# A two-layer graph attention kernel: rows of x stored by turns in layer 1 and loaded in one piece in layer 2, no rows for missing edges in layer 1, and a ring of 29 slots for 28

## The chip, the core and the metric

The kernel runs on one core of a Trainium2 chip. The metric is the device time of one execution in microseconds; the kernel before has a median of 5479.95 us over 14 runs (5473.43 to 5489.02). The names of the engines are those of the profile: PE (TensorE; PEld is its weight load), DVE (VectorE), ACT (ScalarE), POOL (GpSimd) and SP (SyncE, which here only issues DMAs).

## What is computed

Two graph attention layers on 10,000 nodes and 170,000 given edges (each node's self loop is among them, and the reference adds another), then a residual and a normalisation:

```python
def gat_conv(x, edge_index, W, a_src, a_dst, bias, heads, out_ch, concat):
    ei = _add_self_loops(edge_index, n)
    src, dst = (ei[0], ei[1])
    xl = (x @ W).reshape(n, heads, out_ch)
    alpha_src = jnp.einsum('nhc,hc->nh', xl, a_src)
    alpha_dst = jnp.einsum('nhc,hc->nh', xl, a_dst)
    e = jax.nn.leaky_relu(alpha_src[src] + alpha_dst[dst], 0.2)
    # softmax of e over the edges of each dst
    msg = xl[src] * alpha[:, :, None]
    out = jax.ops.segment_sum(msg, dst, num_segments=n)
...
h = gat_conv(x, edge_index, W1, a_src1, a_dst1, b1, 4 heads of 256, True)
h1 = relu(layer_norm(h, g1, be1)) + (x @ Wr1 + br1)
h = gat_conv(h1, edge_index, W2, a_src2, a_dst2, b2, 1 head of 768, False)
out = layernorm(x + layer_norm(h, g2, be2) + (h1 @ Wr2 + br2))
```

x is 10000 x 768, h1 is 10000 x 1024; everything is in float32.

## The kernel before, in words

Three stages follow one another. The first (to 899 us) multiplies x by W1 and writes table1: for each node a row of 1033 numbers, namely 1024 of x @ W1, four logit parts as a source, four as a destination, and one number R1 - 1 that is the node's place in the order below. `prepare` runs between these products. It sorts the nodes by their number of edges, cuts them into 79 tiles of 128, and lists for each tile as many slots as its fullest node needs: slot k of a tile holds, for each of the 128 nodes, the table row of its k-th edge (slot 0 is the node itself). A node with fewer edges has in the slots left over the number of one extra row (`none`), whose logits are -1e30, so that its weight is zero. The tiles have 8 to 41 slots, 1377 in all. `TURNS` is the order of the tiles: every second one from the smallest to the largest, then the others back to small.

Layer 1 (`ordered_layer1`, 899 to 3419 us) goes through the tiles. The rows of a slot come by one indirect DMA from POOL (`gather`, L418, 128 rows) into a ring of RING1 = 28 slots (class `Ring`; `fetch` issues the gather of a slot as soon as the program has weighed the slot that was in its place). `logits` (L467 to L478) adds the source parts of a tile's slots to the destination part, with one DVE instruction for each unbroken stretch of the ring, and takes the exponential on ACT (L475); in layer 1 it then copies the number R1 - 1 of each row into `slots` on ACT (L478), which is the list that layer 2 gathers by. `normalised` (L485 to L491) makes the softmax. The rows are then weighed and summed: the first few slots by PE with diagonal matrices (L709), the others by DVE, one in four wholly (L508) and three in four after ACT has scaled them (L497, then L504). `weights_of(t + 1)` does the next tile's logits and first diagonals before the last LEAD = 3 slots of tile t are weighed, where SLOTS[t + 1] + LEAD fits in the ring. So DVE waits at L467 for the last gather of the next tile with three weighings behind it. Beside this PE transposes the tile's rows of x (L572, which ACT copies out at L575), multiplies them by Wr1, normalises the tile before (L550 to L566, with ACT's square root at L554), and multiplies its h by W2. SP stores the row of layer 2 (table2, L730) and hT (h1_d, L777). The tile's rows of x, 128 x 768, come by a gather by node from POOL (`fetch_x`) into one of two buffers `xt`; it is issued at the end of a tile, for the tile two further on.

Layer 2 (`ordered_layer2`, 3419 to 5475 us) has the same order, with a ring of 38 slots and rows of 770 numbers. A tile's own rows lie together in table2, so slot 0 comes by a direct load from SP (L445) and the others by gathers from POOL. DVE weighs 512 columns (L508), PE the other 256 (L859, L860). `residual(t + 1)` begins the PE work of tile t (L871 takes x, L874 hT); it needs hT, which SP loads from h1_d (L835), and the tile's rows of x, which POOL gathers a second time. Both are asked for in the middle of the weighing of the tile two before. The result is scattered by node (L893) with a bounds check, since the last tile has nodes beyond the 10,000. For the one tile that the ring can't hold whole (41 slots), `attend_parts` works in parts, and the x of the tile two further on is asked for after it.

Each engine runs its instructions in the order in which the program gives them (`manual_schedule`), and POOL and SP issue their DMAs in that order too: a DMA whose wait isn't over holds back all those behind it on the same engine. POOL's DMAs use eight semaphores in turn, so each waits for the one eight before it.

Of the kernel before, what the change touches and what calls it, by code (L numbers as in the profile page):

```python
# [34 lines left out]
P = 128  # L35
# [9 lines left out]
G = 4  # L45
RING1 = 28
RING2 = 38
# [31 lines left out]
def gnn_kernel(ctx, tc, x, x_cols, src, dst, src_col, dst_col, W1, a_src1, a_dst1, b1, g1, be1, Wr1, br1,  # L79
# [27 lines left out]
    res2 = dram.tile([NP, C2], F32, name="res2")  # L107
    h1_d = dram.tile([NT, P, C1], F32, name="h1_d")
    shift = dram.tile([1, C2], F32, name="shift")
    order_d = [dram.tile([NP, 4], I32, name=f"order{i}_d") for i in range(LISTS)]  # L110
# [77 lines left out]
    def prepare():  # L188

        with tc.tile_pool(name="prep", bufs=1, side="right") as pool, \  # L190
# [108 lines left out]
            nc.vector.tensor_sub(base, base, each)  # L299
            rank = pool.tile([P, NT], F32, name="rank")  # L300
            to = pool.tile([P, NT], I32, name="to")
            written = 0
# [34 lines left out]
            with nc.allow_non_contiguous_dma(reason="16 bytes a node"):  # L337
                for to, d in zip([sorted_] + others, order_d):
                    nc.sync.dma_start(to, d.rearrange("(t p) f -> p t f", p=P))
                    yield  # L340
                nc.sync.dma_start(table1[:NP, R1 - 1:].rearrange("(p j) r -> p (j r)", p=P), rank)
                yield
# [91 lines left out]
    class Ring:  # L434

        def __init__(self, pool, table, row, size, own):
            self.table, self.size, self.own, self.issued = table, size, own, 0
            self.rows = pool.tile([P, size, row], F32, name="ring")  # L440

        def fetch(self, upto):
            for q in range(self.issued, min(upto, TOTAL)):
                if q in self.own:
                    nc.sync.dma_start(self.slot(q), self.table[self.own[q] * P:(self.own[q] + 1) * P, :])  # L445
                else:
                    gather(self.slot(q), self.table[:, :], slots[:, q:q + 1])
                self.issued = q + 1
# [12 lines left out]
    def logits(small, ring, lo, hi, ad, heads, c, top=None):  # L461


        n = hi - lo
        e = small.tile([P, ring.size, heads], F32, name="e")[:, :n]
        for a, b, rows in ring.parts(lo, hi):
            nc.vector.tensor_tensor(e[:, a - lo:b - lo], rows[:, :, c:c + heads],  # L467
                                    ad[:, None, :].to_broadcast([P, b - a, heads]), op=OP.add)
# [6 lines left out]
        nc.scalar.activation(e, e, AF.Exp)  # L475
        if not ring.own:
            for a, b, rows in ring.parts(lo, hi):
                nc.scalar.copy(slots[:, a:b], rows[:, :, R1 - 1])  # L478
        return e, new
# [111 lines left out]
    with tc.tile_pool(name="w1", bufs=1) as w1p, tc.tile_pool(name="l1", bufs=2) as io, \  # L591
# [16 lines left out]
        nc.vector.memset(none[:, C1:], -BIG)  # L608
        nc.vector.memset(none[:, R1 - 1:], float(NP))
        nc.scalar.dma_start(table1[NP:NP + 1, :], none)  # L610
# [6 lines left out]
        def weight_steps():  # L617
# [8 lines left out]
            load(w2, W2)  # L626
            for i, a in enumerate((a_src2, a_dst2)):
# [16 lines left out]
        for t in range(NT):  # L644
            p = product(xTs.pop(t), w1, C1)
            row = io.tile([P, R1], F32, name="row")
            nc.scalar.copy(row[:, :C1], p[:, :C1])  # L647
            for i, vec in enumerate((as_b, ad_b)):
                m = io.tile([P, C1], F32, name="scr")
# [18 lines left out]
    def ordered_layer1():  # L668
        nonlocal ps_big
        with tc.tile_pool(name="b1", bufs=1) as pool, tc.tile_pool(name="small1", bufs=2) as small, \  # L670
# [6 lines left out]
            def fetch_x(t):  # L677
                xt = pool.tile([P, D0], F32, name="xt", bufs=2)
                gather(xt, x[:, :], nodes(t))
                return xt  # L680

            xs = {t: fetch_x(t) for t in range(min(2, NT))}
            ring.fetch(RING1)
# [7 lines left out]
            def weights_of(t):  # L691

                n, m = SLOTS[t], on_pe(t)
                e, _ = logits(small, ring, FIRST[t], FIRST[t] + n, ring.slot(FIRST[t])[:, C1 + H1:C1 + 2 * H1], H1, C1)
                yield e
# [36 lines left out]
            for t in range(NT + 1):  # L732
# [47 lines left out]
                if last:  # L780
                    events.append((first + 2, to_layer2))

                def due(k):
                    while events and events[0][0] <= k:
                        events.pop(0)[1]()

                if live and not whole:
                    due(n)
                    acc = ps_acc.tile([P, 2 * BANK], F32, name="acc")
                    ad = small.tile([P, H1], F32, name="ad")  # L790
                    nc.vector.tensor_copy(ad, ring.slot(FIRST[t])[:, C1 + H1:C1 + 2 * H1])
                    attend_parts(small, ring, acc, acc, ad, None, H1, DH1, t)
# [15 lines left out]
                if live:  # L808
                    last = r, acc
                    if t + 2 < NT:  # L810
                        xs[t + 2] = fetch_x(t + 2)
            store(NT - 1)

    def ordered_layer2():
        nonlocal ps_big
        with tc.tile_pool(name="b2", bufs=1) as pool, tc.tile_pool(name="small2", bufs=2) as small, \
# [28 lines left out]
            def weights_of(t):  # L845
# [3 lines left out]
                ad = small.tile([P, H2], F32, name="ad")  # L849
                nc.vector.tensor_add(ad, ring.slot(FIRST[t])[:, C2 + H2:], lift)  # L850
                e, _ = logits(small, ring, FIRST[t], FIRST[t] + n, ad, H2, C2)
# [52 lines left out]
            for t in range(NT):  # L904
# [4 lines left out]
                if not whole(t):  # L909
                    for _ in last:  # L910
                        pass
                    ad = small.tile([P, H2], F32, name="ad")
                    nc.vector.tensor_add(ad, ring.slot(FIRST[t])[:, C2 + H2:], lift)
                    attend_parts(small, ring, h, h, ad, b2_b, H2, DH2, t)
# [33 lines left out]
    def general_path():  # L948
# [82 lines left out]
        def attend_chunks(keep, work, small, lists, table, row, heads, dh, t):  # L1031
# [6 lines left out]
            top = keep.tile([P, heads], F32, name="top")  # L1038
            nc.vector.tensor_copy(top, acc[:, c:c + heads])
# [3 lines left out]
            nc.vector.tensor_copy(adm[:, :heads], acc[:, c + heads:c + 2 * heads])  # L1043
            tmp = small.tile([P, heads], F32, name="tmp")
# [6 lines left out]
            with tc.For_i(lo, hi, G) as i:  # L1051
# [19 lines left out]
                for g in range(0, G, zg):  # L1071
                    z = work.tile([P, zg, heads, P], F32, name="z")
                    nc.vector.tensor_tensor(
                        z, off[:, g:g + zg, None, :].to_broadcast([P, zg, heads, P]),
                        xg[:, g:g + zg, c:c + heads, None].to_broadcast([P, zg, heads, P]), op=OP.add)
                    pz = ps_tr.tile([P, BANK // P, P], F32, name="tr")
# [20 lines left out]
                e = small.tile([P, G, heads], F32, name="ge")  # L1097
                nc.vector.tensor_add(e, xg[:, :, c:c + heads], sel[:, :, :heads])
                leaky(e, e)
# [117 lines left out]
```

## Time and profile before

| | |
|---|---|
| median of 14 runs | 5479.95 us |
| the profiled execution's own time | 5476.48 us |
| its span, first to last instruction | 5474.7 us |
| mean granted TensorE clock | 0.939 |
| busy: PE, DVE, ACT, POOL | 4750.9, 4328.1, 3149.0, 3247.0 us |
| gathers of ring slots (L418) | 2675, mean 969 ns on POOL |
| gathers of x, layer 1 and layer 2 | 79 of mean 966 ns, 79 of mean 963 ns |
| moved by the DMA engines | 1581.74 MB, mean 289 GB/s |

A row of the groups of instructions gives the line, the engine, the operation, what it writes and reads, how often, its busy time and mean duration, and then the idle time of its engine just before such instructions, with those that ended it. A row of the waits gives the waiting instruction, what it waited for, and the sum, number and longest of the waits. In the windows the busy time of each engine is given for a stretch of the span. A POOL row of a gather covers the issuing alone; the transfer follows, and the table of DMA issues gives its median time to landing (5.3 us for the x gathers of layer 1, 5.4 for those of layer 2). The slices of the page show 311 to 366 GB/s through most of both layers.

### The profile page before, as it was taken

What the parts mean: (1) busy time and instruction counts of PE and PEld (TensorE: products, weight loads), DVE (VectorE), ACT (ScalarE), POOL (GpSimd) and SP (SyncE); (2) the same over time, 40 slices, a digit from 0 to 9 for tenths busy, and PEclk for the clock granted to TensorE, in tenths of its full rate; (3) what the DMA queues carried; (4) which work ended last, traced back from release to release, by engine and by line L of the source; (5) the groups of instructions that cost most, each with busy time, mean ns of one, the idle gap of its engine ahead of it and who ended that gap; (6) DMA issues with size and microseconds to landing.
All of it is one profiled execution on the core that took longest, in us unless ns stands there. A gap on an engine that the chain in (4) does not pass through costs nothing. (4 is left out here: it accounts for less than half of the span.)

```text
span 5474.7 us, 58297 instructions
## 1 busy us (share of the span) xinstructions
PE 4750.9 (87%) x15032; PEld 2828.1 (52%) x15032; DVE 4328.1 (79%) x7766; ACT 3149.0 (58%) x8255; POOL 3247.0 (59%) x3238
## 2 busy tenths in 40 slices
PE   9999997999999875478999999799988746888998
PEld 3444443555555543345555555466665524555665
DVE  5784244899988888788999998498887776778998
ACT  3433344788888876688988887244343312333443
POOL 2445465455566555455666553477777775777774
PEclk9999998999999987789999999899988878889999
DMA  4322625899999988789999997699999987999996
GB/s 156 122 95 82 95 92 214 311 328 342 341 357 349 344 314 299 282 322 344 360 366 344 339 324 251 248 347 359 349 331 323 333 293 260 326 325 349 345 361 236
DMA packets 457866, 1581.74 MB, mean 289 GB/s; under 512 B 111851, under 2 KB 116011, under 8 KB 457526
## 3 DMA queue, kind: packets, MB, share of 16 engines
q0 software_dynamic: 328704, 1339.21, 67.9%
q1 hardware_dynamic: 126768, 235.29, 13.0%
q10 hardware_dynamic: 2054, 3.42, 0.2%
q8 instruction: 126, 2.06, 0.1%
q14 instruction: 214, 1.75, 0.1%
HBM read 1431.80 MB, written 146.23 MB: 288 GB/s over the span
## 5 line engine op out<-in xcount | busy, mean ns | idle before, releaser
L418 POOL DMA_INDIRECT ring<-table,slots x2675 | 2591.5, 969 | 1629.4 <-DVE acc L508 404.4
L508 DVE SCALAR_TENSOR_TENSOR acc<-ring,e,acc 128x256 f32<-128x256 f32 (+1 forms) x2538 | 1572.1, 619 | 125.9 <-PE acc L709 50.4
L497 ACT ACTIVATE ring<-ring,e 128x256 f32<-128x256 f32 x3320 | 1351.0, 505 | 0.0
L504 DVE TENSOR_TENSOR acc<-acc,ring 128x1024 f32<-128x1024 f32 x830 | 1022.5, 1232 | 72.8 <-ACT ring L497 1.2
L874 PE MATMUL big<-wr,w 128*128 128x512 f32 (+1 forms) x2528 | 849.9, 489 | 0.0
L169 PE MATMUL big<-w,xT 128*128 128x512 f32 x1896 | 827.1, 598 | 23.4 <-DMA w<-in_W_dram 9.0
L169 PE MATMUL big<-wr,xT 128*128 128x512 f32 x1896 | 835.4, 597 | 0.7 <-ACT xT L575 0.7
L169 PE MATMUL big<-w,hT 128*128 128x512 f32 (+1 forms) x2528 | 832.1, 486 | 1.2 <-ACT hT L575 1.2
L860 PE MATMUL big<-ring,diagonals 128*128 128x256 f32 x2672 | 667.6, 412 | 182.0 <-ACT diagonals L859 174.9
L860 PEld LDWEIGHTS big<-ring,diagonals 128*128 128x128 f32 x2672 | 548.3, 208 | 298.2 <-ACT diagonals L859 198.6
L169 PEld LDWEIGHTS big<-w,hT 128*128 128x128 f32 x2528 | 478.3, 189 | 375.1 <-issue 341.0
L709 PE MATMUL acc<-ring,diagonals 128*128 128x256 f32 x1816 | 452.7, 407 | 242.9 <-ACT diagonals L703 211.6
L874 PEld LDWEIGHTS big<-wr,w 128*128 128x128 f32 x2528 | 484.9, 192 | 345.1 <-issue 312.5
L169 PEld LDWEIGHTS big<-w,xT 128*128 128x128 f32 x1896 | 362.6, 192 | 485.8 <-issue 468.2
L169 PEld LDWEIGHTS big<-wr,xT 128*128 128x128 f32 x1896 | 357.6, 192 | 422.0 <-issue 421.0
L709 PEld LDWEIGHTS acc<-ring,diagonals 128*128 128x128 f32 x1816 | 367.3, 205 | 320.5 <-ACT diagonals L703 230.9
L859 ACT ACTIVATE diagonals<-ident,e 128x128 f32<-128x128 f32 x1336 | 399.9, 387 | 153.6 <-DVE e L488 116.9
L554 ACT ACTIVATE sd<-mv,eps 128x1 f32<-128x1 f32 x237 | 69.8, 294 | 614.2 <-DVE mv L552 613.7
L650 DVE TENSOR_TENSOR scr<-big,as_b 128x1024 f32<-128x1024 f32 x79 | 96.7, 1224 | 388.6 <-ACT row L647 388.6
L655 POOL TENSOR_TENSOR row<-row,none 128x1024 f32<-128x1024 f32 x79 | 187.1, 2368 | 277.8 <-ACT row L647 277.3
L703 ACT ACTIVATE diagonals<-ident,e 128x128 f32<-128x128 f32 x908 | 278.5, 387 | 96.1 <-DVE e L488 96.1
L475 ACT ACT_TABLE_LOAD x153 | 196.3, 1283 | 224.8 <-DVE e L474 197.9
(172 smaller groups left out, 3898.0 us busy)
## 6 DMA issues: line engine op xcount, KB each, us to landing
ring<-table,slots POOLq DMA_INDIRECT x2675, 6.5
table<-row SPq DMA_DIRECT2D x79, 516.0 KB, 3.6
h_d<-hT SPq DMA_DIRECT2D x79, 512.0 KB, 7.3
w<-h_d SPq DMA_DIRECT2D x79, 512.0 KB, 8.3
table<-row SPq DMA_DIRECT2D x79, 385.0 KB, 6.2
ring<-table SPq DMA_DIRECT2D x79, 385.0 KB, 6.5
xT<-in_x_cols_dram SPq DMA_DIRECT2D x79, 384.0 KB, 4.4
wr<-in_Wr_dram SPq DMA_DIRECT2D x2, 3072.0 KB
```

What stands on the lines that cost most here:

```text
L169: nc.tensor.matmul(p[:, c:e], aT[:, j, :], w[:, j, c:e], start=(j == 0), stop=(j == k - 1))
L418: nc.gpsimd.indirect_dma_start(out=to, out_offset=None, in_=table, in_offset=bass.IndirectOffsetOnAxis(ap=index, axis=0), **more)
L475: nc.scalar.activation(e, e, AF.Exp)
L497: nc.scalar.activation(row[:, s], row[:, s], AF.Copy, scale=e[:, h:h + 1])
L504: nc.vector.tensor_add(acc[:, :c], acc[:, :c], row[:, :c])
L508: nc.vector.scalar_tensor_tensor(acc[:, s], row[:, s], e[:, h:h + 1], (acc if first is None else first)[:, s], op0=OP.mult, op1=OP.add)
L655: nc.gpsimd.tensor_add(row[:, :C1], row[:, :C1], b1_b)
L703: nc.scalar.activation(diagonals[:, k * H1 + i, :], ident, AF.Copy, scale=e[:, k, i:i + 1])
L709: nc.tensor.matmul(acc[:, c:d], diagonals[:, k * H1 + i, :], ring.slot(FIRST[t] + k)[:, c:d], start=(k == 0 and c % BANK == 0), stop=(k == ...
L859: nc.scalar.activation(diagonals[:, k % G, :], ident, AF.Copy, scale=e[:, k, :])
L860: nc.tensor.matmul(to, diagonals[:, k % G, :], ring.slot(FIRST[t] + k)[:, ON_PE2:C2], start=False, stop=(k == n - 1), skip_group_check=True)
L874: nc.tensor.matmul(r[:, c:d], hT[:, j, :], wr2[:, j, c:d], start=False, stop=(j == K1 - 1 and (d < C2 or not whole(t))), skip_group_check= ...
```

## The change

Four things, and what they bring with them:

- In layer 1 each tile's rows of x, once gathered, are also stored by SP to a new tensor x_d, in the order of the tiles. Layer 2 loads them from there with one direct DMA from SP, just behind the load of h1_d, and gathers x no more.
- `xt` has one buffer instead of two. The gather of the next tile's x is an event in the middle of the tile, after the slot first + 2 has been weighed; it comes behind the transposes and the store of the rows now in the buffer, and waits for both.
- RING1 is 29.
- In layer 1 the gathers behind the first 29 slots have a bounds check, and a row whose number is beyond the nodes isn't transferred: what the slot held stays there. So that its weight is zero, DVE sets the source logits of every slot to -1e30 once they are read, together with the number R1 - 1, which is therefore stored with its sign turned; the slot list is its negative, at most NP. The two logit parts change places in the row, so that one memset covers both. ACT's copy into `slots` becomes a DVE instruction.

```diff
-RING1 = 28
+RING1 = 29
...
+    x_d = dram.tile([NT, P, D0], F32, name="x_d")
...
+                nc.vector.tensor_scalar(less_rank, rank, -1.0, None, op0=OP.mult)
+                nc.sync.dma_start(table1[:NP, R1 - 1:].rearrange("(p j) r -> p (j r)", p=P), less_rank)
...
                 if q in self.own:
                     nc.sync.dma_start(self.slot(q), self.table[self.own[q] * P:(self.own[q] + 1) * P, :])
+                elif q < self.size or self.own:
+                    gather(self.slot(q), self.table[:, :], slots[:, q:q + 1])
                 else:
-                    gather(self.slot(q), self.table[:, :], slots[:, q:q + 1])
+                    gather(self.slot(q), self.table[:, :], slots[:, q:q + 1], bounds_check=NP - 1,
+                           oob_is_err=False)
...
         nc.scalar.activation(e, e, AF.Exp)
-        if not ring.own:
-            for a, b, rows in ring.parts(lo, hi):
-                nc.scalar.copy(slots[:, a:b], rows[:, :, R1 - 1])
+        for a, b, rows in ring.parts(lo, hi):
+            if not ring.own:
+                nc.vector.tensor_scalar(slots[:, a:b], rows[:, :, R1 - 1], -1.0, float(NP), op0=OP.mult, op1=OP.min)
+                nc.vector.memset(rows[:, :, c + heads:], -BIG)
...
             def fetch_x(t):
-                xt = pool.tile([P, D0], F32, name="xt", bufs=2)
+                xt = pool.tile([P, D0], F32, name="xt")
                 gather(xt, x[:, :], nodes(t))
                 return xt
...
                 if live:
                     xT = pool.tile([P, K0, P], F32, name="xT")
-                    moves = columns(xT, xs[t])
+                    moves = columns(xT, xt)
+                    nc.sync.dma_start(x_d[t], xt)
...
+                def next_x():
+                    nonlocal xt
+                    xt = fetch_x(t + 1)
+
+                if t + 1 < NT:
+                    events.append((first + 2, next_x))
...
                 if live:
                     last = r, acc
-                    if t + 2 < NT:
-                        xs[t + 2] = fetch_x(t + 2)
...
                 nc.sync.dma_start(hT, h1_d[t])
-                gather(xt, x[:, :], nodes(t))
+                nc.sync.dma_start(xt, x_d[t])
```

More of the change, by code (lines that the diff above doesn't have):

```diff
@@ L300, in prepare @@
             rank = pool.tile([P, NT], F32, name="rank")
+            less_rank = pool.tile([P, NT], F32, name="less_rank")
             to = pool.tile([P, NT], I32, name="to")
@@ L340, in prepare @@
                     yield
-                nc.sync.dma_start(table1[:NP, R1 - 1:].rearrange("(p j) r -> p (j r)", p=P), rank)
+                nc.vector.tensor_scalar(less_rank, rank, -1.0, None, op0=OP.mult)
+                nc.sync.dma_start(table1[:NP, R1 - 1:].rearrange("(p j) r -> p (j r)", p=P), less_rank)
                 yield
@@ L466, in logits @@
         for a, b, rows in ring.parts(lo, hi):
-            nc.vector.tensor_tensor(e[:, a - lo:b - lo], rows[:, :, c:c + heads],
+            nc.vector.tensor_tensor(e[:, a - lo:b - lo], rows[:, :, c + heads:c + 2 * heads],
                                     ad[:, None, :].to_broadcast([P, b - a, heads]), op=OP.add)
@@ L608, in gnn_kernel @@
         nc.vector.memset(none[:, C1:], -BIG)
-        nc.vector.memset(none[:, R1 - 1:], float(NP))
         nc.scalar.dma_start(table1[NP:NP + 1, :], none)
@@ L626, in weight_steps @@
             load(w2, W2)
-            for i, a in enumerate((a_src2, a_dst2)):
+            for i, a in enumerate((a_dst2, a_src2)):
                 vec = spread(w1p, a, "a2")
@@ L647, in gnn_kernel @@
             nc.scalar.copy(row[:, :C1], p[:, :C1])
-            for i, vec in enumerate((as_b, ad_b)):
+            for i, vec in enumerate((ad_b, as_b)):
                 m = io.tile([P, C1], F32, name="scr")
@@ L677, in fetch_x @@
             def fetch_x(t):
-                xt = pool.tile([P, D0], F32, name="xt", bufs=2)
+                xt = pool.tile([P, D0], F32, name="xt")
                 gather(xt, x[:, :], nodes(t))
                 return xt
-            xs = {t: fetch_x(t) for t in range(min(2, NT))}
+            xt = fetch_x(0)
             ring.fetch(RING1)
@@ L693, in weights_of @@
                 n, m = SLOTS[t], on_pe(t)
-                e, _ = logits(small, ring, FIRST[t], FIRST[t] + n, ring.slot(FIRST[t])[:, C1 + H1:C1 + 2 * H1], H1, C1)
+                e, _ = logits(small, ring, FIRST[t], FIRST[t] + n, ring.slot(FIRST[t])[:, C1:C1 + H1], H1, C1)
                 yield e
@@ L790, in ordered_layer1 @@
                     ad = small.tile([P, H1], F32, name="ad")
-                    nc.vector.tensor_copy(ad, ring.slot(FIRST[t])[:, C1 + H1:C1 + 2 * H1])
+                    nc.vector.tensor_copy(ad, ring.slot(FIRST[t])[:, C1:C1 + H1])
                     attend_parts(small, ring, acc, acc, ad, None, H1, DH1, t)
@@ L849, in weights_of @@
                 ad = small.tile([P, H2], F32, name="ad")
-                nc.vector.tensor_add(ad, ring.slot(FIRST[t])[:, C2 + H2:], lift)
+                nc.vector.tensor_add(ad, ring.slot(FIRST[t])[:, C2:C2 + H2], lift)
                 e, _ = logits(small, ring, FIRST[t], FIRST[t] + n, ad, H2, C2)
@@ L912, in ordered_layer2 @@
                     ad = small.tile([P, H2], F32, name="ad")
-                    nc.vector.tensor_add(ad, ring.slot(FIRST[t])[:, C2 + H2:], lift)
+                    nc.vector.tensor_add(ad, ring.slot(FIRST[t])[:, C2:C2 + H2], lift)
                     attend_parts(small, ring, h, h, ad, b2_b, H2, DH2, t)
@@ L1038, in attend_chunks @@
             top = keep.tile([P, heads], F32, name="top")
-            nc.vector.tensor_copy(top, acc[:, c:c + heads])
+            nc.vector.tensor_copy(top, acc[:, c + heads:c + 2 * heads])
             total = keep.tile([P, heads], F32, name="total")
@@ L1042, in attend_chunks @@
             adm = keep.tile([P, 2 * heads], F32, name="adm")
-            nc.vector.tensor_copy(adm[:, :heads], acc[:, c + heads:c + 2 * heads])
+            nc.vector.tensor_copy(adm[:, :heads], acc[:, c:c + heads])
             tmp = small.tile([P, heads], F32, name="tmp")
@@ L1074, in attend_chunks @@
                         z, off[:, g:g + zg, None, :].to_broadcast([P, zg, heads, P]),
-                        xg[:, g:g + zg, c:c + heads, None].to_broadcast([P, zg, heads, P]), op=OP.add)
+                        xg[:, g:g + zg, c + heads:c + 2 * heads, None].to_broadcast([P, zg, heads, P]), op=OP.add)
                     pz = ps_tr.tile([P, BANK // P, P], F32, name="tr")
@@ L1097, in attend_chunks @@
                 e = small.tile([P, G, heads], F32, name="ge")
-                nc.vector.tensor_add(e, xg[:, :, c:c + heads], sel[:, :, :heads])
+                nc.vector.tensor_add(e, xg[:, :, c + heads:c + 2 * heads], sel[:, :, :heads])
                 leaky(e, e)
```

## The prediction

> **What bounds the kernel now.** I cut the span into stages first: the product stage ends at 899 us, layer 1 of the attention runs to 3419, layer 2 to 5475. The busy time by window comes first, because the page's averages (DVE 79%, POOL 59%) mix the two layers. Columns: window, length, then busy us (x instructions) of PE, PEld, DVE, ACT, POOL, then PE clock, DMA share, GB/s.
>
> ```profile
> 1035.00:1573.00 538.00, 515.08 (x1724) 303.97 (x1723) 491.39 (x774) 450.13 (x1102) 302.38 (x315) 1.00 0.93 337
> 2036.00:2320.00 284.00, 153.49 (x478) 92.64 (x478) 229.39 (x348) 194.77 (x493) 142.60 (x149) 0.76 0.81 290
> 3736.00:4096.00 360.00, 330.79 (x1155) 223.21 (x1156) 298.43 (x626) 142.89 (x348) 269.85 (x280) 0.96 0.95 347
> 4096.00:4404.00 308.00, 238.83 (x806) 166.24 (x806) 235.32 (x464) 108.06 (x273) 222.65 (x231) 0.87 0.92 326
> 4945.00:5418.00 473.00, 436.11 (x1515) 288.57 (x1516) 427.86 (x915) 205.46 (x490) 358.14 (x372) 0.97 0.96 354
> ```
>
> To see in them: in layer 1 (first row) DVE works 491 us in 774 instructions; its timeline shows 0.04 us between two, so 491 + 31 = 522 of 538: DVE bounds it. In layer 2 POOL looks only 75% busy, but its timeline says otherwise:
>
> ```profile
> 4022.33 0.97 POOL L418 DMA_INDIRECT ring<-table,slots  x1 [0.30 <-PE big L860]
> 4023.61 0.94 POOL L418 DMA_INDIRECT w<-in_x_dram,order  x1 [0.30 <-issue]
> 4024.86 0.95 POOL L418 DMA_INDIRECT ring<-table,slots  x1 [0.30 <-DMA ring<-table,slots]
> ```
>
> A gather is issued every 0.96 + 0.30 = about 1.26 us, whoever is named as the releaser: 0.30 is the floor between two. Then 280 x 1.26 = 353 of 360 us, 231 x 1.26 = 291 of 308, 372 x 1.26 = 469 of 473. POOL's issue of gathers paces layer 2; in layer 1 the same sum gives 397 of 538.
>
> Who pays is in the waits of DVE in layer 2, of the whole program, and in one place of layer 2 (us in total, times, longest):
>
> ```profile
> DVE e L467 <- DMA ring<-table,slots: 166.3, 41, 7.9
> DVE e L491 <- ACT e L475: 41.1, 70, 2.7
> PE big L871 <- DMA w<-in_x_dram,order: 62.8, 1, 62.8
> DVE sd L565 <- ACT sd L554: 26.3, 1, 26.3
> ```
>
> The first: logits wait for the last gather of their tile. With the entries that name a neighbour on the same semaphore the timeline's total at L467 is 223 us in layer 2, and 52 in layer 1. The second hides new DVE work in layer 1. The last two are one event at 4508 to 4565.
>
> **The change, part by part (layer 2).** (1) 79 gathers of x leave POOL: 79 x 1.26 = 100 us of its pace. A tile gains what POOL stops costing, at most its own L467 wait. Tile by tile in the timeline, 47 of 79 wait 1.25 us or more (59 us); the others' waits add 6: 65 us. Where POOL waits for a ring slot (0.5 to 3 us a tile in the larger tiles), the x gather lies between that wait and the tile's last gather, as in the lines above, so it counts there too. A rule speaks against this part: the Trainium skill, "DMA: Bandwidth & Descriptors", section "Issuing engines are not separate DMA queues": the issuing engine changes nothing in the transfer, only its own issue time, "usually small relative to the DMA itself". By it I would book next to nothing. The row gives a pace of 1.26 us of issue beside 1.1 us of transfer (394 KB at 350 GB/s): not small, and eight transfers overlap while issues do not. I take the row. But the rule's first half sets a ceiling: the bytes stay. Page slices never pass 366 GB/s, and that many bytes at 347 GB/s leave 5%, 1.2 us of a 24 us tile. The same page's "Anatomy of one DMA" section divides by 436 GB/s, which would leave 20%; nothing here reaches it, so I use 366. With queues that full, I take 80% of 65: -52 us (ends 0 and -100).
> (2) In their place SP issues 79 loads of 384 KB. Nearest row: the own-row load, 385 KB, 6.5 us to landing beside 5.4 for the gather. SP is idle; behind these loads stand only own-row and h1_d loads, both ahead by a tile. Cost 0.
> (3) The one stall: the largest tile (41 slots) isn't held whole, so the x gather of the tile two further on stands on POOL behind its whole ring, is issued at 4515 and lands at 4519.5. PE waits 62.8 us for it, in order ahead of the next tile's weights; ACT stands behind that, and DVE waits 26.3. On SP it follows the h1_d load (issued at 4488). PE's 12 us of residual are then over near 4512, the 27 diagonals follow (10 us), so the 4540 of DVE becomes about 4521: -19 us (ends -10 and -25).
> (4) At the start of layer 2 two gathers fewer stand ahead of the second tile's: -2.5.
>
> Layer 2: -73.5.
>
> **Layer 1.** (5) DVE gets two instructions per stretch of the ring that a tile covers: 124 stretches with 29 slots (130 with 28). The slot numbers: nearest row, TENSOR_SCALAR 128x4, 174 ns. The memset of some 75 elements, between 66 ns (1x9) and 912 (128x1024): 0.12. With two gaps 0.375 us each time: 124 x 0.375 - 6 x 0.2 = 45 us. They stand between L474 and L491, where DVE waits for ACT's exp: 0.53 us in most tiles. A tile of one stretch is covered, a tile of two pays 0.22; without cover it pays all. Tile by tile: +17 (ends +10 and +45). ACT loses 130 casts of 0.2 us, off the path. Its multiplies now each carry a wait for the slot's DMA, already over when DVE passed L467:[...] 0.
> (6) One more slot: the last gather of the next tile is issued one weighing earlier, 1.5 us. Taking at most 1.5 us of each L467 wait from the 23rd tile to the 53rd: -28 (ends 0 and -50). The tile of 26 slots can now be weighted ahead (26 + 3 = 29): -2. PE's order is the same.
> (7) Skipped rows: 6,144 of 176,256 slots are empty by the inputs, 5,212 behind the first 29 slots: 21.5 MB. In some 19 tiles the whole last slot is empty, and logits wait for one gather less: -3. The bounds check: the scatter that has one takes 1,028 ns beside 966; POOL has 5 to 15 us of slack a tile in layer 1: +3 at most through the critical gather.
> (8) The store of x adds 31 MB, net +10 MB, unevenly: tiles without empty slots get 0.39 MB more. At 18 slots 11.2 MB / 366 = 30.7 us against 30.3 now: +8 over the ten or so tiles near that.
> (9) The x gather is issued inside the tile and waits on POOL for the store of the row before. Behind it stand ring gathers. By the timeline of the tile that begins at 1513, its store would follow the row store at 1523, 10 us into the tile, and land at 16 (6.2 us, the row store's median, same size). POOL gets there at 15.5, after the third weighing: a stall under 1 us in 5 us of slack: 0. Only the start pays: x of the second tile moves from the 10th to the 35th place on POOL (899 + 34 x 1.25 = 941.6, landing near 951), while PE took it at 938 and ACT at 941.6. PE was then idle for 5 us: +7 (ends 0 and +15).
>
> Layer 1: +17 - 28 - 2 - 3 + 3 + 8 + 7 = +2. In the product stage one DVE instruction of 0.2 us: 0.
>
> **Sum.** -71.5 on the profiled execution's own 5476.5 us: 5405. The median of the runs stands 3.5 above that execution: 5408.
>
> **Rivals.** *Full pace*: layer 2 takes all 65 and the ring gives more than its 28 (up to 42, three us a tile). Layer 2 -87, layer 1 -12 or better: about 5375, to 5345. For: the middle of layer 2 moves only 326 GB/s. *Transfers take over*: at 347 to 354 GB/s in the outer tiles the 16 engines are 95% busy, and what POOL saves is lost as later landings. Left are the stall and the start, -21.5, and +2: about 5460. Against: slices of 361 GB/s exist in layer 2. *POOL waits for the store* (the slower side): if in layer 1, under 337 to 360 GB/s, stores take t us to land, each tile stalls POOL t - 5.5 us; beyond some 5.5 us of slack the 79 tiles pay. It cancels the gain from t = 5.5 + 5.5 + 73.5/79 = 12 us; at 13 us each pays 2 us, -71.5 + 158: 5566. Against: the issue table has 6.2 us as the median of such a store, and 7.3 for the larger one of h1. *The skip isn't made* (the empty rows still move): +6 us and 5414, inside the forecast.
>
> **Chances.** Forecast (5385 to 5440) 0.60, full pace 0.20, transfers take over 0.14, POOL waits for the store 0.06. Within 0.2% (5469 to 5491) is what a measurement of this kernel can't tell from no change; a third of the third case reaches it. Faster 0.90, same 0.04, slower 0.06. The range 5345 to 5465 leaves out the slower rival and the edge of the third.
>
> **What would show it.** POOL's gather count in layer 2 falls by 79 and its issue floor stays 1.25 us; L467 waits fall from 223 to about 150; the 62.8 us wait of PE is gone; DVE's wait at L491 in layer 1 is near 0 and its busy time up 45 us; GB/s in layer 2 rises to about 360. Wrong, if L467 waits keep their size with landings over 7 us (transfers), or if POOL waits over 2 us at each x gather in layer 1 (the store).

## The result and the profile after

The changed kernel takes 5409.01 us (median of 6 runs, 5406.60 to 5411.45), beside 5479.82 us for the kernel before (28 runs): a ratio of 0.9872, 95% interval 0.9862 to 0.9881. That is 71 us less; the forecast was 5408. The profiled execution took 5405.4 us, with a span of 5403.6 and a clock of 0.943.

The same stretches of work as those of the prediction, now a little earlier in the span (columns as there). Left out is one row, of layer 1:

```profile
1046.00:1584.00 538.00, 514.83 (x1724) 303.80 (x1723) 497.63 (x830) 446.83 (x1071) 320.89 (x315) 1.00 0.95 346
...
3723.00:4069.00 346.00, 329.09 (x1162) 224.00 (x1160) 298.41 (x626) 143.46 (x349) 255.90 (x263) 0.97 0.97 361
4069.00:4372.00 303.00, 237.68 (x804) 165.66 (x804) 235.73 (x466) 108.05 (x273) 211.99 (x220) 0.88 0.93 330
4885.00:5345.00 460.00, 437.83 (x1539) 294.71 (x1538) 428.74 (x918) 206.38 (x490) 339.71 (x347) 0.97 0.98 367
```

In layer 1 (first row) 538 us are 538 us still, with 56 more instructions of DVE. In layer 2 the outer stretches are 14 us shorter of 360 and 13 of 473, and move 361 and 367 GB/s where they moved 347 and 354; the middle one is only 5 us shorter of 308. POOL has 17, 11 and 25 instructions fewer there. Its floor between two gathers is the old one:

```profile
4006.72 0.94 POOL L421 DMA_INDIRECT ring<-table,slots  x1 [0.30 <-issue]
4007.97 0.95 POOL L421 DMA_INDIRECT ring<-table,slots  x1 [0.30 <-issue]
4009.22 0.95 POOL L421 DMA_INDIRECT ring<-table,slots  x1 [0.30 <-PE big L887]
```

The waits of DVE from 3560 to 5340 us (the prediction's 166.3 us row is of the same tiles):

```profile
DVE e L474 <- DMA ring<-table,slots: 158.5, 39, 10.2
DVE e L474 <- issue: 18.6, 5, 5.4
DVE sd L573 <- ACT sd L562: 10.1, 5, 5.4
```

By the first row the logits' wait has hardly fallen, and its longest has grown from 7.9 to 10.2 us. With the entries under other names the timeline's total at this line went from 230 to 190 us in layer 2 (the prediction had 223, and expected about 150) and from 52 to 30 in layer 1. A wait of the same size was one half of the prediction's sign that transfers take over; landings over 7 us were the other, and the new load of x lands 10.8 us after its issue (under e). What lies behind that is told there. The square root's waits fell from 37.4 us to 10.1: that is the one stall.

To place the gain I cut the span at the exponentials of the tiles (the starts of ACT's exp in the timeline; tiles in the order of the program; us from exp to exp, from each kernel's one profiled execution). The experiments stand in the same table:

| | L1: 0-2 | 2-28 | 28-50 | 50-78 | L2: to 25 | 25-40 | 40-41 | 41-54 | 54 to the end |
|---|---|---|---|---|---|---|---|---|---|
| before | 36.8 | 744.3 | 924.1 | 795.0 | 596.6 | 492.3 | 57.3 | 380.1 | 529.4 |
| after | 46.3 | 744.6 | 902.5 | 795.1 | 581.6 | 486.6 | 36.5 | 373.1 | 517.9 |
| a, x by turns alone | 38.7 | 747.3 | 937.2 | 798.8 | 581.2 | 486.6 | 38.1 | 374.9 | 517.8 |
| b, layer 1 alone | 45.2 | 744.7 | 892.1 | 795.5 | 595.0 | 490.0 | 57.8 | 376.8 | 529.9 |
| c, filler on POOL | 46.1 | 744.1 | 900.4 | 796.0 | 603.0 | 502.8 | 36.4 | 384.5 | 539.2 |
| d, no x load | 46.3 | 743.9 | 899.9 | 794.8 | 577.5 | 477.2 | 36.3 | 365.2 | 516.1 |
| e, x from ACT's queue | 46.4 | 745.0 | 905.0 | 796.4 | 577.6 | 477.2 | 40.5 | 365.6 | 513.0 |
| k, the same, before the exp | 46.5 | 744.5 | 898.4 | 795.4 | 577.5 | 481.8 | 39.3 | 370.1 | 512.1 |
| f, no skip | 46.3 | 745.0 | 908.8 | 796.2 | 583.3 | 485.4 | 36.6 | 373.9 | 518.7 |
| g, ring of 28 | 44.0 | 748.2 | 924.7 | 800.1 | 585.7 | 488.1 | 36.1 | 372.3 | 518.2 |
| h, second x early | 38.7 | 743.9 | 900.4 | 796.1 | 585.2 | 485.5 | 38.0 | 374.7 | 516.1 |
| i, new work twice | 46.3 | 746.9 | 902.3 | 799.1 | 579.4 | 486.1 | 36.5 | 375.8 | 517.5 |
| j, e and h | 38.8 | 743.6 | 899.9 | 794.7 | 576.4 | 476.9 | 39.3 | 364.9 | 514.4 |
| l, j with h1 from ACT too | 38.9 | 744.7 | 901.1 | 796.2 | 579.0 | 456.6 | 39.6 | 350.5 | 515.4 |

Where the code of a stage is the same, rows differ by up to 7 us in L1 28-50, 6 in L2 to 25 and 4 in the others; for all of layer 1 that is 8 us (2484.8 to 2492.7) and for all of layer 2 it is 5 (1995.2 to 2000.5). Layer 1 gained 11.8 us (2500.3 to 2488.5; predicted +2), layer 2 60 (2055.7 to 1995.7; predicted -73.5). So the sum was right and its two halves were not.

### The profile page after: what moved, and what is told of

Its sections match the earlier page's. It is cut to its first block, busy times and chain, and to the rows that moved or that the text cites. A ratio compares the mean times of both kernels' runs of the same rounds, so it can differ in the third digit from the quotient of the medians.

```text
span 5403.6 us, 59675 instructions
## 1 busy us (share of the span) xinstructions
PE 4731.5 (88%) x15032; PEld 2823.5 (52%) x15032; DVE 4352.3 (81%) x8008; ACT 3136.0 (58%) x8125; POOL 3240.5 (60%) x3159
## 5 line engine op out<-in xcount | busy, mean ns | idle before, releaser
L421 POOL DMA_INDIRECT ring<-table,slots x2675 | 2661.8, 995 | 1503.3 <-DVE acc L516 356.9
L657 DVE TENSOR_TENSOR scr<-big,ad_b 128x1024 f32<-128x1024 f32 x79 | 96.7, 1224 | 390.4 <-ACT row L654 390.4
L660 ACT ACTIVATE scr<-scr 128x256 f32<-128x256 f32 x632 | 253.6, 403 | 123.0 <-DVE scr L657 123.0
```

The lines of the kernel that those rows point to most:

```text
L421: nc.gpsimd.indirect_dma_start(out=to, out_offset=None, in_=table, in_offset=bass.IndirectOffsetOnAxis(ap=index, axis=0), **more)
L660: nc.scalar.activation(m[:, s], m[:, s], AF.Copy, accum_out=row[:, C1 + i * H1 + h:C1 + i * H1 + h + 1])
```

## The experiments

The theories at the start: POOL's issue paces layer 2 and the new loads are free (the prediction); against it, the loads of x from SP cost something, or POOL was only waiting for what it was spared. The lines shown are against the kernel before in a, against e in k, against j in l, and against the changed kernel in the others. The changed kernel's ratio to compare with is 0.9872.

**a, x by turns alone.** The kernel before, with x stored in layer 1 and loaded in layer 2; ring, gathers, buffers of x and slot lists as before.

```diff
                     moves = columns(xT, xs[t])
+                    nc.sync.dma_start(x_d[t], xs[t])
...
                 nc.sync.dma_start(hT, h1_d[t])
-                gather(xt, x[:, :], nodes(t))
+                nc.sync.dma_start(xt, x_d[t])
```

> The kernel before with one part of the change alone: layer 1 also stores its rows of x (31 MB, two buffers for x as before), and layer 2 loads them by SP instead of gathering them; the ring of 28 slots, all rows and the numbers of a row as before. The changed kernel took 71 us off, 60 of them in layer 2 and 12 in layer 1. If layer 2 owes its 60 us to this part (79 gathers of 1.25 us off POOL and the one long wait for x), this kernel keeps them and pays some 3 to 8 us of layer 1 for the store: 5420 to 5430 us. If layer 2 gained by something else (the ring or the skipped rows leaving it a better start), it stands within 10 us of the 5480 before.

Measured: 5445.11 us, ratio 0.9941 (0.9927 to 0.9954). Layer 2 takes 1998.7 us: all of the gain there, within 3 us, comes from this part. But layer 1 pays 21.7 us, more than expected, 13 of them in tiles 28 to 50.

**b, layer 1 alone.** The changed kernel without the store and with layer 2's gather of x.

```diff
-                    nc.sync.dma_start(x_d[t], xt)
...
-                nc.sync.dma_start(xt, x_d[t])
+                gather(xt, x[:, :], nodes(t))
```

> The changed kernel without that part: layer 2 gathers x from POOL again and nothing is stored; one buffer for x, the ring of 29 slots, the skipped rows and the new DVE instructions stay. By the theory that the two parts are independent it should take before less what layer 1 gained, about 12 us, and 3 to 8 more without the store: 5460 to 5468 us, with layer 2 at its old 2056 us. If layer 1 alone costs time, as its 45 us of new DVE work would without cover, it is over 5480.

Measured: 5453.98 us, ratio 0.9957 (0.9944 to 0.9971). Layer 1 gains 22.7 us in spite of its late start (32 in tiles 28 to 50 alone), which is more than expected; layer 2 keeps its old pace (2049.5). Against b the changed kernel's store costs 10.9 us in layer 1; by itself (a) it cost 21.7. By medians against the kernel before on the same chip (5478.23) a gives -33 and b -24, together -57, where the change gave -71. The 14 us between fit a store that costs less with the skip and the larger ring (21.7 - 10.9 = 11 by the stages); no run took those two apart.

**c, a filler in the place of the gather.** Four memsets (`FILLS` = 4) on POOL where the x gather was issued; nothing waits for them.

```diff
                 nc.sync.dma_start(xt, x_d[t])
+                for _ in range(FILLS):
+                    nc.gpsimd.memset(filler, 0.0)
```

> The changed kernel with four memsets of a small tile on POOL at each place in layer 2 where the x gather stood: about the same time of POOL, no transfer, and the load on SP as well. Outputs are unchanged. If layer 2 is paced by the issue of gathers everywhere (theory 1, the prediction's), what layer 2 gained outside the one long wait, about 39 us, is lost again: 5445 to 5450 us. If in the larger tiles it is the transfers ahead of the last gather that count, and POOL only waits for what it was spared (theory 2), only the tiles at both ends lose, 20 to 25 us: 5430 us.

Measured: 5476.41 us, ratio 0.9997 (0.9988 to 1.0006). POOL's timeline of this kernel in layer 2 shows the price of a set:

```profile
4043.16 0.97 POOL L423 DMA_INDIRECT ring<-table,slots  x1 [0.30 <-issue]
4044.13 1.44 POOL L853 MEMSET filler<- 128x256 f32 x4
4045.99 0.95 POOL L423 DMA_INDIRECT ring<-table,slots  x1 [0.42 <-PE big L878]
```

From the end of one gather to the start of the next it is 1.86 us instead of 0.30, so a tile's set costs 1.56 us, a little more than the 1.25 of a gather. It takes 70 us of layer 2 (1995.7 to 2065.9), in every stage but the one stall. That is more than either theory had named, because the net 39 us of theory 1 held a cost of the new load as well (d). The memsets do not slow DVE beside them: its weighing of 512 columns takes 752 ns on the average in both kernels. So POOL's issue time is on the path all through layer 2, and the idea that POOL only waits for what it was spared falls.

**d, no x load.** What it leaves out is told in its expectation.

```diff
-                nc.sync.dma_start(xt, x_d[t])
+                if t < 2:
+                    nc.sync.dma_start(xt, x_d[t])
```

> The changed kernel with x loaded in layer 2 for the first two tiles only: the later tiles use these rows again, so the residual isn't computed from their own x. It leaves out 77 transfers of 384 KB. Theory 1 (POOL's pace): the load cost nothing, 5409 us within 5. Theory 2 (the load of x comes in one burst with the own rows and h1, 8 to 15 us ahead of the last gather of the next tile, and delays it by 0.39 MB at 350 GB/s, 1.1 us): some 30 larger tiles gain 1.1 us each, 5375 to 5385 us, and the L474 waits of DVE in layer 2 fall by as much.

Measured: 5376.94 us, ratio 0.9816 (0.9803 to 0.9830). The loads that I had at nothing cost 32 us by the medians and 23 in the profiled layer 2, 17 of them in tiles 25 to 40 and 41 to 54. In those tiles the change had won 5.7 and 7.0 us; without the load it would have won 15.1 and 14.9.

**e, the same load from ACT's queue, behind the next tile's exp.** The bytes are those of the changed kernel; only the issue moves. The load behind the largest tile stays on SP.

```diff
-                nc.sync.dma_start(xt, x_d[t])
+                if t < 2:
+                    nc.sync.dma_start(xt, x_d[t])
...
+            def load_x2(t, queue=None):
+                (queue or nc.scalar).dma_start(parts[2 + t % 2][:, :D0], x_d[t])
...
                             ready += itertools.islice(ahead, 1)
+                        if k == min(turn, n - 1) and t + 2 < NT:
+                            load_x2(t + 2)
```

> Leaves nothing out. In layer 2 the load of x (from the third tile on) is issued from ACT's queue at the step of the tile where ACT turns to the next tile's diagonals, instead of from SP together with the own-row load and the h1 load; the one behind the largest tile stays on SP. Bytes are the same. Theory 1 (the load costs its bytes: transfers share the 16 engines, wherever the load is issued): 5405 to 5412, as the changed kernel, and the 20 tiles of layer 2 around the middle keep their pace. Theory 2 (the load costs by its moment: three loads in one burst lie ahead of the next tile's last gather): some of the 32 us that leaving the load out saved comes back, 5380 to 5397. Theory 3 (the moment was right, ACT is the wrong place: the load waits on ACT behind its diagonals and PE waits for x): 5420 or more, with PE waiting for x at the residual.

Measured: 5383.04 us, ratio 0.9824 (0.9810 to 0.9837): 26 us of the 32 come back, and every stage of layer 2 but the one stall is within 0.4 us of d or below it. So the load costs by when or where it is issued, and not by its bytes. One tile of the changed kernel: SP's queue, then the last gather of the next tile on POOL, DVE's wait for it, and the exp:

```profile
4111.15 0.32 SPq L449 DMA_DIRECT2D ring<-table  x1
4111.52 0.42 SPq L848 DMA_DIRECT2D w<-h_d  x1
4112.04 0.38 SPq L849 DMA_DIRECT2D w<-x_d  x1
...
4116.88 0.94 POOL L421 DMA_INDIRECT ring<-table,slots  x1 [0.30 <-issue]
...
4125.12 0.19 DVE L474 TENSOR_TENSOR e<-ring,ad 128x20 f32<-128x20 f32 x1 [5.55 <-DMA ring<-table,slots]
...
4125.97 0.22 ACT L482 ACTIVATE e<-e 128x20 f32<-128x20 f32 x1 [5.61 <-DVE e L481]
```

The same tile in e, on ACT and its queue:

```profile
4119.45 0.22 ACT L482 ACTIVATE e<-e 128x20 f32<-128x20 f32 x1 [4.19 <-DVE e L481]
4119.53 0.33 ACTq L854 DMA_DIRECT2D w<-x_d  x1
```

In the changed kernel SP issues 385 + 512 + 384 KB within 1.3 us, 14 us ahead of the next exp; the last gathers that this exp waits for are issued behind them, the very last at 4116.88, and DVE waits 5.55 us for it. In e, x goes out 0.08 us after the start of an exp, and the gathers for the one after it have most of a tile's time. The DMA issues of tiles 25 to 38 (the last column is the median us from issue to landing), of the changed kernel and of e:

```profile
w<-h_d SPq DMA_DIRECT2D x14, 512.0 KB, 8.3
w<-x_d SPq DMA_DIRECT2D x14, 384.0 KB, 10.8
```

```profile
w<-x_d ACTq DMA_DIRECT2D x14, 384.0 KB, 5.5
```

And DVE's waits of e from 3560 to 5340, against 158.5 and 18.6 before this edit:

```profile
DVE e L474 <- DMA ring<-table,slots: 129.1, 38, 9.8
DVE e L474 <- issue: 14.5, 4, 5.6
```

**k, the load from ACT's queue, but ahead of the exp.** As e, with the two statements exchanged, so that ACT issues the load as soon as it is done with its diagonals.

```diff
+                        if k == min(turn, n - 1) and t + 2 < NT:
+                            load_x2(t + 2)
                         if k in (turn, turn + LEAD):
                             ready += itertools.islice(ahead, 1)
-                        if k == min(turn, n - 1) and t + 2 < NT:
-                            load_x2(t + 2)
```

> Leaves nothing out: as the kernel with x on ACT's queue, but the load stands one instruction earlier in ACT's order, ahead of the next tile's exp instead of behind it. ACT doesn't wait for that tile's last gather then and issues the load while that gather is still to come. Theory 2 (what counts is that the load lies ahead of the next tile's last gather): the gain is lost again in part or whole, 5395 to 5412. Theory 4 (what counted was the burst of three on SP, or the queue): the gain stays, 5379 to 5390.

Measured: 5388.20 us, ratio 0.9828 (0.9815 to 0.9841), which cannot be told from e. The time lies in the range of theory 4. The stages say more: tiles 25 to 40 take 4.6 us longer than in e and tiles 41 to 54 4.5, about half of the 17 us that e had won in them. For these two stages together, rows of the same code differ by at most 3 us. The other stages are e's. The rows of k for the tile shown above, the tile's last gather on POOL and then ACT and its queue:

```profile
4109.00 0.95 POOL L421 DMA_INDIRECT ring<-table,slots  x1 [0.30 <-issue]
...
4110.23 0.33 ACTq L854 DMA_DIRECT2D w<-x_d  x1
...
4117.80 0.22 ACT L482 ACTIVATE e<-e 128x20 f32<-128x20 f32 x1 [5.32 <-DVE e L481]
```

The load now lies 7.6 us ahead of the exp, but it is not ahead of the critical gather as theory 2 had it: in this tile it is issued 1.2 us behind it, and in tiles 25 to 38 1.1 us behind it (median), while that gather is still on its way. So in the middle tiles about half of the price is paid when the load only travels beside the critical gather (one profile of each kernel). The other half, and the outer tiles, may be that SP's load goes out ahead of that gather (2.6 us, median of the same tiles), the burst of three, or the queue. Which of them stays open: no run issued x alone from SP at another moment.

**l, the h1 load behind the exp as well.** On top of j (below), ACT issues h1 and then x there.

```diff
-                nc.sync.dma_start(hT, h1_d[t])
-                if t < 2:
+                if t < 2:
+                    nc.sync.dma_start(hT, h1_d[t])
                     nc.sync.dma_start(xt, x_d[t])
...
             def load_x2(t, queue=None):
+                (queue or nc.scalar).dma_start(parts[t % 2], h1_d[t])
                 (queue or nc.scalar).dma_start(parts[2 + t % 2][:, :D0], x_d[t])
```

> Leaves nothing out: both amendments, and the h1 load (512 KB) is issued behind the exp on ACT's queue as well, ahead of x. By theory 2 the h1 load ahead of the critical gather costs as x's did, by its bytes some 30 us in layer 2: 5335 to 5350. Rival (one load can hide behind the exp, two end up ahead of the gather after that, or PE waits for them at its residual): 5365 to 5380, or slower.

Measured: 5343.54 us (5340.50 to 5344.41), ratio 0.9747 (0.9733 to 0.9760): the fastest of all, 26 us below j. Tiles 25 to 40 and 41 to 54 lose 20.3 and 14.4 us against j; the outer ones gain nothing. That load was in the kernel before, on SP, where it cost about as much as x's did (30.7 us of layer 2, beside 23). DVE's waits of l from 3560 to 5340:

```profile
DVE e L474 <- DMA ring<-table,slots: 102.8, 40, 7.6
...
DVE e L474 <- issue: 11.2, 6, 3.7
```

In l both loads come in one burst, but behind the exp, and x lands later than in e. The issues of x in tiles 25 to 38, of k and then of l:

```profile
w<-x_d ACTq DMA_DIRECT2D x13, 384.0 KB, 7.1
```

```profile
w<-x_d ACTq DMA_DIRECT2D x14, 384.0 KB, 8.9
```

So a late landing of the load itself costs nothing here. What changes is the critical gather: from its issue to the exp that needs it, tiles 25 to 38 take 9.05 us (mean) in the changed kernel, 8.84 in k, 8.49 in e and 6.97 in l. Times the 14 tiles, e is 8 us below the changed kernel and l another 21 below e, about what the stage 25-40 shows. In e and l the load of x is issued some 19 us ahead of that gather and has landed long before it starts.

**f, no skip.** The bounds check of layer 1's gathers is taken away, and the rows of missing edges move again.

```diff
-                elif q < self.size or self.own:
-                    gather(self.slot(q), self.table[:, :], slots[:, q:q + 1])
                 else:
-                    gather(self.slot(q), self.table[:, :], slots[:, q:q + 1], bounds_check=NP - 1,
-                           oob_is_err=False)
+                    gather(self.slot(q), self.table[:, :], slots[:, q:q + 1])
```

> Leaves nothing out: the changed kernel with the bounds check of layer 1's gathers taken away, so that the rows of missing edges are moved again (the row behind the table, of zeros), 21.5 MB more; ring, memsets and the store of x stay. Prediction's term: the empty rows are worth 6 us, its bounds check costs up to 3: 5412 to 5418. Rival (the skip pays for the bytes of the store: 31 MB stored against 21.5 MB skipped): layer 1 loses about as much as the store costs by itself, 10 to 20 us: 5420 to 5430, most of it in the tiles of 15 to 27 slots. Rival (the skip is worth nothing because tiles wait for full rows anyway): 5409 within 4.

Measured: 5415.22 us, ratio 0.9891 (0.9876 to 0.9907); layer 1 loses 7.8 us, 6.3 in tiles 28 to 50. That is at the edge of what can be told: in both, f stands 4 us above the slowest row with the changed kernel's layer 1 (2492.7 and 905.0). The prediction's rival without the skip said 5414. Ring gathers of layer 1 from 950 to 3380 us, the changed kernel and f:

```profile
L421 POOL DMA_INDIRECT ring<-table,slots x1340 | 1360.3, 1015 | 915.3 <-DVE acc L516 246.3 <-DVE acc L512 157.0 <-issue 133.7
```

```profile
L421 POOL DMA_INDIRECT ring<-table,slots x1339 | 1294.2, 967 | 996.0 <-DVE acc L513 265.9 <-DVE acc L509 214.6 <-PE acc L713 134.9
```

The bounds check costs POOL 1015 - 967 = 48 ns a gather, some 65 us in all, and none of it shows in the time, which is the shorter with it: in layer 1 POOL has slack.

**g, a ring of 28.** `RING1 = 28`, nothing else.

> Leaves nothing out: the changed kernel with 28 slots in layer 1's ring instead of 29. By the prediction's term the slot is worth 28 + 2 us, in the tiles from the 23rd to the 53rd: 5437 to 5442. Rival (the gain of layer 1 came from the skip and from DVE's shorter wait for ACT, and the slot is worth little): 5412 to 5420.

Measured: 5435.41 us, ratio 0.9922 (0.9909 to 0.9936): the slot is worth 26 us. Layer 1 loses 28.5, 22.2 of them in tiles 28 to 50.

**h, x of the second tile early.** It is gathered before the rest of the ring, as in the kernel before, into the buffer of `h`, which is idle until that tile.

```diff
             xt = fetch_x(0)
+            xt_second = pool.tile([P, C1], F32, name="h")[:, :D0]
+            gather(xt_second, x[:, :], nodes(1))
             ring.fetch(RING1)
...
-                    xt = fetch_x(t + 1)
+                    xt = fetch_x(t + 1) if t else xt_second
```

> Leaves nothing out: the changed kernel with x of layer 1's second tile gathered before the ring's remaining slots, as in the kernel before, into a buffer that lies idle until that tile's end. Theory (the start pays because this gather stands behind some 25 ring gathers on POOL): the first tiles give back 7 to 10 us, 5399 to 5402, and the exp of the third tile comes 9 us earlier. Rival (the delay at the start is made up by the ring being filled earlier, so that it is given back in the tiles after): 5406 to 5409.

Measured: 5397.24 us, ratio 0.9853 (0.9838 to 0.9868). The first stage gives back 7.6 us and nothing takes them again. PE's timeline at the start of layer 1, the changed kernel and then h (where these rows are in the tile named h):

```profile
952.65 1.51 PE L580 MATMUL big<-ident,xt 128*128 128x128 f32 x6 [13.44 <-DMA xt<-in_x_dram,order]
```

```profile
940.34 0.82 PE L580 MATMUL big<-ident,h 128*128 128x128 f32 x6
```

**i, DVE's new work twice.** Each stretch of layer 1's ring gets both new instructions a second time.

```diff
                 nc.vector.memset(rows[:, :, c + heads:], -BIG)
+                nc.vector.tensor_scalar(slots[:, a:b], slots[:, a:b], 1.0, float(NP), op0=OP.mult, op1=OP.min)
+                nc.vector.memset(rows[:, :, c + heads:], -BIG)
```

> Leaves nothing out: the changed kernel with DVE's two new instructions per stretch of layer 1's ring (slot numbers, reset of the logits) made twice, 248 instructions more, some 37 us of their own time and 10 us of gaps. Theory A (the first set cost nothing because it filled DVE's wait for ACT's exp, of which some 5 us are left): the second set has no cover and pays its whole time in layer 1's tiles that DVE bounds, 5430 to 5455. Theory B (new work of DVE lies in other slack, the wait for the tile's last gather or beside the instruction before it): much less, 5411 to 5422.

Measured: 5417.16 us, ratio 0.9887 (0.9872 to 0.9902), as theory B had it. In the two stages that DVE bounds (2-28 and 50-78) i takes 6.3 us more than the changed kernel, where the rows of its code differ by 3. DVE's timeline of i, a tile of two stretches:

```profile
1260.74 0.37 DVE L485 TENSOR_SCALAR slots<-ring 128x8 int32<-128x8 f32 x1
1261.19 0.09 DVE L486 MEMSET ring<- 128x40 f32 x1
1261.19 0.13 DVE L487 TENSOR_SCALAR slots<-slots 128x8 int32<-128x8 int32 x1
1261.36 0.09 DVE L488 MEMSET ring<- 128x40 f32 x1
1261.36 0.13 DVE L485 TENSOR_SCALAR slots<-ring 128x7 int32<-128x7 f32 x1
```

L485 and L486 are the first set, L487 and L488 the second. A memset starts together with the instruction after it: a second set takes 0.17 us from start to start, 21 us for 124 stretches. About a third of that shows in the stages; so some of it is covered even now.

**j, e and h together.**

> Leaves nothing out: both amendments together, layer 2's loads of x from ACT's queue and layer 1's second x gathered early. If their gains (26 and 12 us below the changed kernel) lie in different stages and add: 5368 to 5376.

Measured: 5369.55 us, ratio 0.9798 (0.9784 to 0.9811). The two gains add (26 + 12 = 38 below the changed kernel, 39 measured).

## Why the prediction was right in its sum, step by step

**(1) The gathers off POOL: predicted -52; the mechanism holds, and the size was too small.** From the kernel before to d, layer 2 falls by 83.4 us. Less the stall (21.0) that is 62 us, nearly all of the 65 that the logits waited. Kernel e, which still moves the rows of x, gives 81.8 - 16.8 = 65 us, so this is POOL's part and not that of the bytes. The 80% that I took for full queues was the error: I read 366 GB/s, the highest slice, as a ceiling. The rule of the Trainium skill that I used for it ("DMA: Bandwidth & Descriptors", section "Issuing engines are not separate DMA queues": the issuing engine changes nothing in the transfer) says what moves, not how fast: a DMA busy share of 0.95, as in the windows of before, left room. Its other half, an issue time "usually small relative to the DMA itself", does not hold for these gathers: 1.56 us a tile cost 70 us (c). The eight overlapping transfers in my reason were too many, though: with a median landing of 4.9 us (tiles of the middle, before) and one gather in 1.26 us, about four overlap. The outer stretches went to 361 and 367 GB/s, and one slice of the changed kernel to 381:

```profile
GB/s 155 125 98 77 98 89 184 305 331 343 354 366 362 360 334 283 266 335 345 370 368 354 353 334 322 191 336 374 367 345 329 336 296 304 339 334 355 365 381 215
```

l brings the same bytes through layer 2 in 54 us less. Only the outer tiles, where l gains nothing over j, may be near a limit of transfers; no run settles that.

**(2) The loads on SP: predicted 0; this is the step that failed.** They cost 23 us of layer 2 (32 by the medians, d). I asked what stands behind them on SP and found nothing, which was right, but not what they meet in the transfers: the next tile's last gather, for which DVE waits and which is issued 2.6 us behind x (median of tiles 25 to 38). Issued behind an exp, from ACT's queue, the same loads cost nothing that d and e can tell apart (e). The net of (1) and (2) is -39 where -52 was forecast.

**(3) The one stall: predicted -19, measured -20.8.** PE's wait in the kernel before, then the DMA queue of SP and PE's wait in the changed kernel:

```profile
4519.60 2.05 PE L871 MATMUL big<-w,ident 128*128 128x512 f32 x2 [62.77 <-DMA w<-in_x_dram,order]
```

```profile
4421.40 34.26 SPq L449 DMA_DIRECT2D ring<-table  x2
4455.76 0.38 SPq L848 DMA_DIRECT2D w<-h_d  x1
4456.24 0.38 SPq L849 DMA_DIRECT2D w<-x_d  x1
4456.71 0.38 SPq L848 DMA_DIRECT2D w<-h_d  x1
4457.15 0.54 SPq L849 DMA_DIRECT2D w<-x_d  x1
```

```profile
4465.34 2.05 PE L884 MATMUL big<-w,ident 128*128 128x512 f32 x2 [52.10 <-DMA w<-x_d]
```

PE still waits 52 us for x, so the row that I expected to vanish didn't. But the wait ends 10.7 us ahead of tile 40's exp (4476.1), where it ended 11.7 us behind it before (4519.60 against 4507.9). DVE waits 5.4 us at the square root instead of 26.3. A long wait is not a cost; its end is.

**(4) The start of layer 2: predicted -2.5.** Its first tiles (78 to L2's 3) went from 129.0 to 128.6 us: next to nothing, and less than rows of the same code differ (128.6 to 130.2).

**(5) DVE's new work: predicted +17, measured 0.** Over tiles 2 to 28 the span is the same (744.3 and 744.6) with 80 instructions more (40 stretches), and the waits of DVE over 0.1 us fall by 10.5 us (49.3 to 38.8), nearly all at the softmax behind the exp (12.2 to 1.7). So a stretch takes 10.5 / 40 = 0.26 us and not 0.375, because the memset starts beside its neighbour (by the timeline, 0.25 us lie on the average between the start of L485 and that of the memset behind it), and two stretches fit into the 0.53 us that a tile waited. DVE's busy time in the whole program rose by 24 us (4328.1 to 4352.3), where the forecast had 45 with the gaps. ACT's multiplies, with their new waits, take 506 ns as against 505. The whole of layer 1 shows the cover that is left, beside 41.1 us before:

```profile
DVE e L499 <- ACT e L482: 9.8, 19, 2.3
```

**(6) The slot: predicted -28 and -2, measured -26 (g; -28.5 in the profiled layer 1).** **(7) The skip with its bounds check: predicted 0, measured -6 to -8 (f), hardly clear of the spread.** **(8) The store: predicted +8, measured +10.9 (b; 7 to 15 with the other rows of the changed kernel's layer 1); +21.7 without skip and larger ring (a).** Its waits on POOL, which the slower rival rested on, are there in the changed kernel, in 21 tiles, 3 us each on the average:

```profile
POOL xt L421 <- DMA x_d<-xt: 63.7, 21, 23.8
```

Kernel b has no such waits and is 10.9 us faster in layer 1; whatever the 63.7 us cost is within that. **(9) The start of layer 1: predicted +7, measured +9.5, and h takes 7.6 of it away.** PE got x of the second tile at 952.65 as worked out (951).

So layer 1 is 0 - 26 - 7 + 11 + 9.5 = -12.5 (measured -11.8; with a spread of 8 us the match is closer than it had to be), and layer 2 is -62 + 23 - 21 = -60 (measured -60; it must come out, since -62 and 23 are both taken from d). That the forecast was right to 1 us was luck: the errors had opposite signs. They are these: in layer 2 the loads cost 23 us that were not booked, against 10 that POOL's relief gave above its -52; in layer 1 the 17 us booked for DVE were not paid. Of the rivals, "transfers take over" fell with e and l, which move the same bytes faster; "full pace" had the right size for POOL's part and missed the loads' price.

## What to carry to other kernels

When a transfer moves to another queue, ask what it will travel ahead of or beside, not only what stands behind it on the queue: issue a large load just after the point that the critical transfers have passed (here behind the exp that waits for them), and it may cost nothing. An engine whose issuing paces a stage is worth relieving though it looks 75% busy, and whether a removed issue was on the path is shown by a filler of about the same length in its place. When a sum of several terms is right, test its terms: here two of them were wrong by 23 and 17 us. Following up the first, and the start of layer 1, was worth another 65 us (l against the changed kernel).

## What the runs showed that I had not expected

The same 384 KB land 10.8 us after their issue when they are third in a burst, 7.1 us when issued alone ahead of the exp, 5.5 us alone behind it and 8.9 us second in a burst behind it. The last of these is in the fastest kernel: what counts is what the load travels ahead of or beside, and not when it lands itself. A bounds check costs 48 ns of POOL's issue per gather. And small DVE instructions overlap: a memset of 35 to 40 elements begins at the same time as the instruction after it, so that a tensor_scalar and a memset take 0.17 us from start to start and not the sum of their durations and gaps.
